# Two heads' attention outputs leave PSUM in one pass instead of two

## The chip, the cores and the metric

The kernel runs on one core of a Trainium2 chip. The metric is the device time of one execution in microseconds; the result is given as the median of several runs. Five engines work side by side, each through its own queue in program order: PE (matrix products into PSUM), DVE (vector), ACT (scalar and activations), POOL (a second, slower vector engine) and SP, which here only issues DMAs. PSUM has eight banks of 512 float32 columns per partition; PE writes its products there, and DVE and ACT read them.

## The reference, cut to what matters

The input x is 1024 x 512. After a layer norm it goes through attention and, beside it, through a gated feed-forward network with 4-bit weights; the result is `x + attention * silu(feed-forward)`. The attention has 32 query heads of 128 columns, which share 8 key and value heads (four query heads each), an RMS norm on queries and keys, and a causal mask with a linear bias:

```
q, k, v = (x @ Wq.T), (x @ Wk.T), (x @ Wv.T)      # 32, 8 and 8 heads of 128
scores  = rmsnorm(q) . rmsnorm(k) / sqrt(128) + slope[head] * (j - i)   # j <= i
attn    = softmax(scores)
out     = (attn . v, all heads side by side) @ Wo.T
```

## The kernel before, in words

To keep float32 accuracy with float16 products, nearly every operand is split into a high and a low float16 half, and a product becomes three: high x high, high x low, low x high (`mm3`, lines 112 to 116, so all such products show as L114, L115 and L116).

The kernel has three stages. The first two, the feed-forward network and the projections of queries, keys and values, take the first half of the span. The third is the attention, and the change lies in it. It works through eight groups g (one key and value head and its four query heads each). Within a group there are four blocks of 256 queries, `qb`; `ORDER` takes them as 2, 3, 0, 1, the first group as 3, 2, 1, 0 and the last as 2, 3, 1, 0. A block has four heads, and one head in one block of queries is a *unit* u, 128 in all, so units 4b to 4b+3 are the heads of block b. Each unit has two tiles of 128 queries, `qt`. Because of the causal mask a tile of block `qb` sees (2 qb + qt + 1) x 128 keys: 128 and 256 in block 0, up to 896 and 1024 in block 3.

The order of the work is written out by hand in `step(n)`, and each engine gets its instructions in that order. Step n takes tile n of the list (unit n // 2, tile n % 2) and the earlier tiles at fixed lags:

- `scores` on PE, tile n, into one of two double banks (tag "s");
- `heads_hi` on ACT, for the unit whose last product with the values was issued one step earlier, that is unit u in step 2u + 11;
- `exponentials`, tile n - 1: on DVE L878 adds the bias to the scores and finds the row extreme, on ACT L879 takes the exponential;
- `split_hi`, tile n - 3: ACT L898 scales the probabilities and rounds them to float16;
- `split_lo`, tile n - 4: DVE L907 makes the low half, and SP issues the DMA (L915, for block 0 L910) that transposes both halves into `pT`;
- `heads_lo` on DVE, for the same unit as `heads_hi`;
- `accumulate` on DVE (L980 mostly), which adds a finished output projection to y;
- `values` on PE, tile n - 9 (`AV_LAG`): the products of `pT` with the values into a bank `av` (tag "o", two banks), with parts of the output projection `out_proj` in between.

So unit u's products with the values are issued in steps 2u + 9 and 2u + 10. `values` takes a new bank when part 0 begins and uses its first 256 columns. In step 2u + 11 the head leaves: `heads_hi` (L941, ACT) writes the float16 half `oh`, 128 x 256, and `heads_lo` (L946, DVE) the remainder `ol`. Both come from pools of `OH_BUFS` = 8 buffers. The output projection of a block whose first unit is u0 begins in step 2u0 + 18 with head 0 and takes one head per step.

Other work shares the queues: the output weights come by DMA (L834), are scaled by POOL (L837), rounded by ACT (L843) and their remainder made by POOL (L844).

Of the kernel before, what the change touches and what calls it, by code (L numbers as in the profile page):

```python
# [12 lines left out]
F16 = mybir.dt.float16  # L13
BF16 = mybir.dt.bfloat16
I32 = mybir.dt.int32
AF = mybir.ActivationFunctionType
ALU = mybir.AluOpType
# [4 lines left out]
P = 128  # L22
# [12 lines left out]
QB = 256  # L35
# [3 lines left out]
P_SCALE = 2.0**14  # L39
# [25 lines left out]
GATE_SUMS = [227, 235, 251, 259]  # L65
PF_BUFS = 5
P16_BUFS = 5
OH_BUFS = 8

_START = 2 ** (-(2 ** (-(math.log2(H) - 3))))  # L70
SLOPES = np.array([_START * _START**i for i in range(H)], dtype=np.float32)
# [5 lines left out]
def attention_gated_by_ffn_kernel(ctx, tc, x, gu_w, gu_z, gu_s, dn_w, dn_z, dn_s, wq, wkv, wo, qnw, knw, out):  # L77
    nc = tc.nc
    ve, se, ge, te, sp = nc.vector, nc.scalar, nc.gpsimd, nc.tensor, nc.sync
# [5 lines left out]
    def ps2(name):  # L85
        return psum[0].tile([P, 2, 512], F32, tag="s", name=name)

    def ps1(tag, name):
        return psum[0].tile([P, 512], F32, tag=tag, name=name)
# [22 lines left out]
    def mm3(ps, lhs, rhs, first, last):  # L112
        (lh, ll), (rh, rl) = lhs, rhs
        te.matmul(ps, lhsT=lh, rhs=rh, start=first, stop=False)  # L114
        te.matmul(ps, lhsT=lh, rhs=rl, start=False, stop=False)  # L115
        te.matmul(ps, lhsT=ll, rhs=rh, start=False, stop=last)  # L116
# [360 lines left out]
    def finish_step():  # L477

        for f in finishing.pop(clock[0], ()):
            f()  # L480
        clock[0] += 1
# [310 lines left out]
    blocks = [(g, qbs) for g in range(HKV) for qbs in (FIRST_ORDER if g == 0 else ORDER if g < HKV - 1 else LAST_ORDER)]  # L792
    units = [(g, qb, hh) for g, qbs in blocks for hh in range(NH) for qb in qbs]
    kT, vT, qT, woh, wol = {}, {}, {}, {}, {}
    trel, pT, oT, wor = {}, {}, {}, {}

    def load_keys(g):
        kT[g] = ap1.tile([P, NT, 2, P], F16, tag="kT", name=f"kT{g}")
        sp.dma_start(kT[g].rearrange("p t a k -> p t (a k)"), kd[g // 2][:, g % 2])

    def load_values(g):
        vT[g] = ap1.tile([P, NT, 2, HD], F16, tag="vT", name=f"vT{g}")
        sp.dma_start(vT[g].rearrange("p t a d -> p t (a d)"), vd[g])

    def load_queries(g, qb):
        qT[g, qb] = ap1.tile([P, NQT, 2, NH, P], F16, tag="qT", name=f"qT{g}_{qb}", bufs=2)
        sp.dma_start(
            qT[g, qb].rearrange("p t a g q -> p t (a g q)"), qd[g][qb * NQT : (qb + 1) * NQT].rearrange("t p c -> p t c")
        )
# [3 lines left out]
    def last_queries(t):  # L813
        g, qb = HKV - 1, t // NQT
        if (g, qb) not in qT:
            qT[g, qb] = ap1.tile([P, NQT, 2, NH, P], F16, tag="qT", name=f"qT{g}_{qb}", bufs=2)
        sp.dma_start_transpose(
            qT[g, qb][:, t % NQT].rearrange("p a g q -> p (a g) q"), last_pairs.pop(t).rearrange("p a g d -> p (a g d)")
        )
# [26 lines left out]
    def relative(g):  # L846

        rel = trel[g] = ap1.tile([P, S], F32, tag="trel", name=f"trel{g}")
        if g == 0:
            ge.iota(rel, pattern=[[-1, S]], base=S - P, channel_multiplier=1, allow_small_or_imprecise_dtypes=True)  # L850
            ge.affine_select(rel, rel, pattern=[[-1, S]], compare_op=ALU.is_ge, fill=1e20, base=S - P, channel_multiplier=1)
            ge.tensor_scalar(rel, rel, rc, float(SLOPES[NH - 1]), ALU.mult, ALU.mult)
        else:
            ge.tensor_scalar(rel, trel[g - 1], float(SLOPES[g * NH + NH - 1] / SLOPES[g * NH - 1]), None, ALU.mult)

    s_ps, pf, rows16, p16, av_ps, op_ps = {}, {}, {}, {}, {}, {}

    def scores(u, qt):
        g, qb, hh = units[u]
        w = (NQT * qb + qt + 1) * P  # L860
        ps = ps2(f"s{u}_{qt}").rearrange("p a c -> p (a c)")
        q = qT[g, qb][:, qt]
        for c0 in range(0, w, 512):
            c1 = min(w, c0 + 512)
            kt = kT[g][:, c0 // P : c1 // P]
            mm3(ps[:, c0:c1], (q[:, 0, hh, :], q[:, 1, hh, :]), (kt[:, :, 0, :], kt[:, :, 1, :]), True, True)
        s_ps[u, qt] = ps[:, :w]
# [51 lines left out]
    def values(u, part, between):  # L919
        g, qb, hh = units[u]  # L920
        nk = NQT * (qb + 1)
        if part == 0:
            av_ps[u] = ps1("o", f"av{u}")[:, :QB]
        ps = av_ps[u]
        per = nk // NQT
        for kt in range(part * per, part * per + per):
            if kt % per == per - 1:
                between()
            c0 = max(0, kt - NQT * qb) * P
            mm3(  # L930
                ps[:, c0:],
                (vT[g][:, kt, 0, :], vT[g][:, kt, 1, :]),
                (pT[u][:, kt, 0, c0:], pT[u][:, kt, 1, c0:]),
                kt == 0,
                kt == nk - 1,
            )

    def heads_hi(u):
        oh = late[0].tile([P, QB], F16, tag="oh", name=f"oh{u}", bufs=OH_BUFS)
        ol = late[0].tile([P, QB], F16, tag="ol", name=f"ol{u}", bufs=OH_BUFS)  # L940
        se.activation(oh, av_ps[u], AF.Copy, scale=1.0 / P_SCALE)  # L941
        oT[units[u]] = (oh, ol)

    def heads_lo(u):
        oh, ol = oT[units[u]]
        ve.scalar_tensor_tensor(ol, av_ps.pop(u), 1.0 / P_SCALE, oh, ALU.mult, ALU.subtract)  # L946

    final = blocks[-1][0], blocks[-1][1][0]

    def out_proj(g, qb, i, part):  # L950
        if part == 0:
            op_ps[g, qb, i] = last_ps[i] if (g, qb) == final else ps1("m", f"op{g}_{qb}_{i}")
        oh, ol = oT[g, qb, part]
        cols = slice(i * P, i * P + P)
        mm3(op_ps[g, qb, i], (oh[:, cols], ol[:, cols]), (woh[g, part], wol[g, part]), part == 0, part == NH - 1)
# [36 lines left out]
    for k, (g, qbs) in enumerate(blocks[:-1]):  # L992
# [5 lines left out]
        n, taken, done = max(free, due), 0, 0  # L998
        op_first.setdefault(g, n)
        for qb in qbs:  # L1000
            for i in range(NQT):
                for part in range(NH):
# [3 lines left out]
                    taken, done = taken + 1, done + 1  # L1006

                    if taken == 2 or n < due + done:
                        n, taken = n + 1, 0
        free = n + (taken > 0)  # L1010
    late, y_ = [], []
    TILES = NT * len(projections)

    def at(n):

        return order[n] if 0 <= n < nn else None

    def step(n):
        nonlocal last_ps
        if n < nn:  # L1020
            u, qt = order[n]
            g, qb, hh = units[u]
            for due in q_at.get(n, ()):
                if due[0] < HKV - 1:
                    load_queries(*due)
            for t, due in LAST_QUERIES.items():
                if due == n:
                    last_queries(t)
            if g + 1 < HKV:
                if n % (NB * BS) == KEYS_STEP:  # L1030
                    relative(g + 1)
                    load_keys(g + 1)
                elif n % (NB * BS) == VALUES_STEP:
                    load_values(g + 1)
            scores(u, qt)
        done = at(n - AV_LAG - 1)
        done = done[0] if done and done[1] == NQT - 1 else None
        if done is not None:
            heads_hi(done)
        for stage, lag in ((exponentials, 1), (split_hi, NQT + 1), (split_lo, NQT + 2)):  # L1040
            if at(n - lag):
                stage(*at(n - lag))
        if done is not None:
            heads_lo(done)
        if n < nn + AV_LAG + 1:
            for due in acc_at.get(n, ()):
                accumulate(*due)
        finish_step()

        def project():  # L1050
            for due in op_at.get(n, ()):
                out_proj(*due)

        if at(n - AV_LAG):
            values(*at(n - AV_LAG), project)
        else:
            project()
        if done is not None and units[done][:2] == final:
            g, qb, hh = units[done]
            if hh == 0:  # L1060
                last_ps = [ps2(f"op_last{i}")[:, 0, :] for i in range(NQT)]
            for i in range(NQT):
                out_proj(g, qb, i, hh)
            if hh == NH - 1:
                for due in acc_at.get(nn + AV_LAG + 1, ()):
                    accumulate(*due, other=True)
                for i in range(NQT):
                    accumulate(g, qb, i)
        if n in GATE_LOADS:
            gate_load(LAST_ORDER[GATE_LOADS.index(n)][0])  # L1070
        for i in range(NQT):
            if n - i in GATE_SUMS:
                gate_partial(LAST_ORDER[GATE_SUMS.index(n - i)][0], i)
        for lead, act in ((WO_SPLIT, split_wo), (WO_SCALE, scale_wo), (WO_LOAD, load_wo)):
            for g, first in op_first.items():
                if n + lead - first in range(0, 2 * NH, 2):
                    act(g, (n + lead - first) // 2)
# [75 lines left out]
```

## Time and profile before

| | |
|---|---|
| three runs, median (lowest to highest) | 1066.62 us (1066.06 to 1070.48) |
| the profiled execution's own time | 1066.42 us |
| its span, first to last instruction | 1064.6 us |
| busy: PE, DVE, ACT, POOL | 1002.7, 886.1, 802.7, 413.9 us |
| exits on ACT, L941 | 128 of 128 x 256, 373 ns each, 47.7 us in all |
| exits on DVE, L946 | 128 of 128 x 256, 418 ns each, 53.5 us in all |
| first and last L941 | 501.2 and 1056.2 us |
| granted clock of PE | 0.993 |

The profile records for every instruction its start and duration, and for idle time before it which event ended it. Its views are a page with shares and slices, groups of instructions by line and shape, windows (busy time of each engine in a stretch), lists of waits, and timelines. Times are counted from the start of the span. An engine's record of an instruction can reach into the next one's, because they are pipelined; where that matters, one counts from start to start. Idle time of an engine that nobody waits for costs nothing.

### The profile page before, as it was taken

The numbers are of one execution on the slowest core, as the hardware profiler recorded it, in microseconds if no ns is written. First come the engines' busy times: TensorE is split into PE (matmuls) and PEld (weight loads), VectorE is DVE, ScalarE is ACT, GpSimd is POOL, SyncE is SP. The second block draws the span as 40 slices with busy tenths as digits, with TensorE's granted clock in tenths as the row PEclk, the third lists the DMA queues.
The fourth block names the chain that finished last, engine by engine and source line by source line (L and its number), as shares of the span: only waits on it lengthen the run. The fifth ranks groups of instructions, "written<-read, shape, count | busy, mean of one in ns | idle before, by whom it ended". The sixth has DMA issues, their size and how long they took to land.

```text
span 1064.6 us, 18405 instructions
## 1 busy us (share of the span) xinstructions
PE 1002.7 (94%) x5913; PEld 584.6 (55%) x5913; DVE 886.1 (83%) x1745; ACT 802.7 (75%) x2160; POOL 413.9 (39%) x407
## 2 busy tenths in 40 slices
PE   7899899999989999898799999999999999999986
PEld 4344377844444444344566666566666666665563
DVE  7888996638778687788799899898998998979986
ACT  5777644778877787587778788797987888868862
POOL 2588653124545546361343215123141141250732
PEclk9999999999999999999999999999999999999998
DMA  6123259447988989989999999899999998999995
GB/s 202 49 100 119 70 170 302 166 139 162 219 228 188 242 203 235 279 179 207 226 193 214 195 200 222 167 227 197 189 207 193 197 223 182 221 224 194 231 189 129
DMA packets 455039, 204.39 MB, mean 192 GB/s; under 512 B 401506, under 2 KB 411038, under 8 KB 454942
## 3 DMA queue, kind: packets, MB, share of 16 engines
q1 hardware_dynamic: 454942, 203.21, 85.4%
q8 instruction: 46, 0.75, 0.3%
q14 instruction: 51, 0.42, 0.1%
HBM read 77.32 MB, written 27.27 MB: 98 GB/s over the span
## 4 chain that ended last, share of the span: by engine, by line
PE 48%; DVE 17%; ACT 13%; issue 10%; DMA 8%; SPq 2%; POOL 2%; DVEq 0%; ACTq 0%; POOLq 0%
PE gu_ps L267 6%; DMA pT<-p 4%; PE s L114 4%; DVE pf L878 3%; PE s L116 3%; PE s L115 3%; PE op L114 3%; PE op L115 3%; PE av L114 3%; PE op L116 3%; PE av L116 3%; PE av L115 3%; ACT p L898 2%; ACT pf L879 2%; PE ps_q L114 2%
## 5 line engine op out<-in xcount | busy, mean ns | idle before, releaser
L907 DVE SCALAR_TENSOR_TENSOR p<-pf,row,p 128x1024 f16<-128x1024 f32 (+7 forms) x256 | 227.8, 890 | 23.5 <-ACT p L898 20.3
L879 ACT ACTIVATE pf<-pf,row 128x1024 f32<-128x1024 f32 (+7 forms) x256 | 197.6, 772 | 57.2 <-DVE row L878 52.7
L878 DVE CUSTOM_DVE_ANT_0 pf<-s,trel,cs 128x1024 f32<-128x1024 f32 (+7 forms) x256 | 207.2, 809 | 13.7 <-PE s L116 13.4
L898 ACT ACTIVATE p<-pf,row 128x1024 f16<-128x1024 f32 (+7 forms) x256 | 196.5, 768 | 8.4 <-DMA pT<-p 3.5
L114 PE MATMUL av<-pT,vT 128*128 128x256 f16 (+1 forms) x640 | 167.8, 262 | 15.5 <-DMA pT<-p 15.5
L115 PE MATMUL av<-pT,vT 128*128 128x256 f16 (+1 forms) x640 | 167.8, 262 | 0.0
L116 PE MATMUL av<-pT,vT 128*128 128x256 f16 (+1 forms) x640 | 167.6, 262 | 0.0
L114 PE MATMUL s<-kT,qT 128*128 128x512 f16 (+3 forms) x384 | 125.0, 325 | 12.4 <-DVE row L878 12.1
L115 PE MATMUL s<-kT,qT 128*128 128x512 f16 (+3 forms) x384 | 125.0, 326 | 0.0
L116 PE MATMUL s<-kT,qT 128*128 128x512 f16 (+3 forms) x384 | 123.4, 326 | 0.0
L837 POOL TENSOR_SCALAR wor<-wor,rvs 128x512 f32<-128x512 f32 x32 | 54.5, 1702 | 162.8 <-DMA wor<-in_wo 141.5
L114 PE MATMUL ps_q<-wh_q,xth 128*128 128x512 f16 x256 | 97.6, 381 | 2.6 <-DVE am_q L526 2.5
L116 PE MATMUL ps_q<-wh_q,xtl 128*128 128x512 f16 x256 | 97.5, 381 | 0.0
L115 PE MATMUL ps_q<-wl_q,xth 128*128 128x512 f16 x256 | 97.5, 381 | 0.0
L114 PE MATMUL op<-woh,oh 128*128 128x512 f16 x248 | 94.5, 381 | 0.0
L115 PE MATMUL op<-wol,oh 128*128 128x512 f16 x248 | 94.3, 380 | 0.0
L116 PE MATMUL op<-woh,ol 128*128 128x512 f16 x248 | 94.2, 380 | 0.0
L114 PEld LDWEIGHTS <-vT 128*128 128x128 f16 x640 | 62.6, 98 | 56.6 <-DMA pT<-p 9.4
L115 PEld LDWEIGHTS <-vT 128*128 128x128 f16 x640 | 62.6, 98 | 41.3 <-issue 3.5
L941 ACT ACTIVATE oh<-av 128x256 f16<-128x256 f32 x128 | 47.7, 373 | 48.5 <-PE av L116 47.8
L636 POOL TENSOR_TENSOR f_q<-f_q,inv_q 128x512 f32<-128x512 f32 x64 | 77.4, 1237 | 1.1
L844 POOL TENSOR_TENSOR wol<-wor,woh 128x512 f16<-128x512 f32 x32 | 49.4, 1543 | 71.3 <-ACT woh L843 71.3
(194 smaller groups left out, 2255.6 us busy)
## 6 DMA issues: line engine op xcount, KB each, us to landing
qd<-tr_q SPq DMA_DIRECT2D x56, 256.0 KB, 3.4
qT<-qd SPq DMA_DIRECT2D x28, 512.0 KB, 4.5
wq<-in_wq SPq DMA_DIRECT2D x32, 256.0 KB, 3.9
wo_sq<-in_wo SPq DMA_DIRECT2D x8, 1024.0 KB, 9.1
wor<-in_wo SPq DMA_DIRECT2D x32, 256.0 KB, 3.7
gui<-in_gu_w SPq DMA_DIRECT2D x13, 512.0 KB, 3.5
wkv<-in_wkv SPq DMA_DIRECT2D x16, 256.0 KB, 3.8
vd<-v SPq DMA_DIRECT2D x8, 512.0 KB, 4.0
```

Source lines behind the costliest of these rows:

```text
L114: te.matmul(ps, lhsT=lh, rhs=rh, start=first, stop=False)
L115: te.matmul(ps, lhsT=lh, rhs=rl, start=False, stop=False)
L116: te.matmul(ps, lhsT=ll, rhs=rh, start=False, stop=last)
L267: te.matmul(banks[j][:, k, :], lhsT=w[:, j, ws], rhs=x[:, j, k * 512 : k * 512 + 512], start=x is xth, stop=x is xtl)
L636: ge.tensor_tensor(f, f, ib, ALU.mult)
L837: ge.tensor_scalar(wor[g, i], wor[g, i], rvs[:, g : g + 1], None, ALU.mult)
L844: ge.tensor_tensor(wol[g, i], raw, woh[g, i], ALU.subtract)
L878: ve.tensor_tensor_reduce(p, ps, trel[g][:, S - w :], cs[:, hh : hh + 1], 3e38, ALU.add, ALU.min, least[:, c])
L879: se.activation(p, p, AF.Exp, bias=least[:, c], scale=-1.0, accum_out=total[:, c])
L898: se.activation(p16[u, qt][:, :, 0, :], pf[u, qt], AF.Copy, scale=scale[:, qt : qt + 1])
L907: ve.scalar_tensor_tensor(lo, p, scale, hi, ALU.mult, ALU.subtract)
L941: se.activation(oh, av_ps[u], AF.Copy, scale=1.0 / P_SCALE)
```

## The change

Two heads of a block, an even unit and the odd one after it, now share a bank: the even unit's product goes to columns 0 to 255, the odd one's to columns 256 to 511. They leave together, after the odd unit's product is done, with one ACT and one DVE instruction of 512 columns each; the even unit's exit in its own step is gone. The four units of the very last block (`final`) stay single, each in a bank of its own with 256 columns. The buffers of `oh` and `ol` become pairs, 6 of 512 columns instead of 8 of 256. `heads_hi` now returns the DVE instruction as a function, which `step` calls where `heads_lo` stood.

```
-OH_BUFS = 8
+OH_BUFS = 6
...
     def values(u, part, between):
...
-        if part == 0:
-            av_ps[u] = ps1("o", f"av{u}")[:, :QB]
-        ps = av_ps[u]
+        if part == 0 and opens(u):
+            av_ps[u] = ps1("o", f"av{u}").rearrange("p (i q) -> p i q", i=2)
+        ps = av_ps[u][:, 0] if opens(u) else av_ps[u - 1][:, 1]
...
+    final = blocks[-1][0], blocks[-1][1][0]
+
+    def opens(u):
+        return u % 2 == 0 or units[u][:2] == final
+
     def heads_hi(u):
-        oh = late[0].tile([P, QB], F16, tag="oh", name=f"oh{u}", bufs=OH_BUFS)
-        ol = late[0].tile([P, QB], F16, tag="ol", name=f"ol{u}", bufs=OH_BUFS)
-        se.activation(oh, av_ps[u], AF.Copy, scale=1.0 / P_SCALE)
-        oT[units[u]] = (oh, ol)
-
-    def heads_lo(u):
-        oh, ol = oT[units[u]]
-        ve.scalar_tensor_tensor(ol, av_ps.pop(u), 1.0 / P_SCALE, oh, ALU.mult, ALU.subtract)
+        n = 1 if opens(u) else 2
+        oh = late[0].tile([P, 2, QB], F16, tag="oh", name=f"oh{u}", bufs=OH_BUFS)[:, :n]
+        ol = late[0].tile([P, 2, QB], F16, tag="ol", name=f"ol{u}", bufs=OH_BUFS)[:, :n]
+        ps = av_ps.pop(u + 1 - n)[:, :n]
+        se.activation(oh, ps, AF.Copy, scale=1.0 / P_SCALE)
+        for i in range(n):
+            oT[units[u + 1 - n + i]] = (oh[:, i], ol[:, i])
+        return lambda: ve.scalar_tensor_tensor(ol, ps, 1.0 / P_SCALE, oh, ALU.mult, ALU.subtract)
...
-        if done is not None:
-            heads_hi(done)
+        heads = done is not None and (done % 2 or units[done][:2] == final)
+        if heads:
+            heads_lo = heads_hi(done)
         for stage, lag in ((exponentials, 1), (split_hi, NQT + 1), (split_lo, NQT + 2)):
             if at(n - lag):
                 stage(*at(n - lag))
-        if done is not None:
-            heads_lo(done)
+        if heads:
+            heads_lo()
```

More of the change, by code (lines that the diff above doesn't have):

```diff
@@ L936, in values @@
             )
+    final = blocks[-1][0], blocks[-1][1][0]
+    def opens(u):
+        return u % 2 == 0 or units[u][:2] == final
     def heads_hi(u):
-        oh = late[0].tile([P, QB], F16, tag="oh", name=f"oh{u}", bufs=OH_BUFS)
-        ol = late[0].tile([P, QB], F16, tag="ol", name=f"ol{u}", bufs=OH_BUFS)
-        se.activation(oh, av_ps[u], AF.Copy, scale=1.0 / P_SCALE)
-        oT[units[u]] = (oh, ol)
-    def heads_lo(u):
-        oh, ol = oT[units[u]]
-        ve.scalar_tensor_tensor(ol, av_ps.pop(u), 1.0 / P_SCALE, oh, ALU.mult, ALU.subtract)
-    final = blocks[-1][0], blocks[-1][1][0]
+        n = 1 if opens(u) else 2
[6 more added lines that the diff above has]
+        return lambda: ve.scalar_tensor_tensor(ol, ps, 1.0 / P_SCALE, oh, ALU.mult, ALU.subtract)
     def out_proj(g, qb, i, part):
```

## The prediction

> **What bounds the kernel now.** I read the page first: engine shares, and the span in 40 slices.
>
> ```profile
> PE   7899899999989999898799999999999999999986
> DVE  7888996638778687788799899898998998979986
> ```
>
> The change touches only the attention stage, from the first heads at 501 us to the end: the right half, where PE and DVE both stand near full. So next came the windows of one of its eight groups, group 3, cut at the steps where its key width changes (768, 1024, 256, 512 columns).
>
> ```profile
> 685.50:702.00 16.50, 16.50 (x117) 10.47 (x116) 16.21 (x35) 15.07 (x33) 2.76 (x1) 1.00 1.05 207
> 702.00:725.10 23.10, 23.10 (x159) 14.63 (x158) 22.43 (x38) 19.82 (x35) 10.33 (x6) 1.00 1.07 218
> 725.10:741.30 16.20, 15.23 (x125) 11.27 (x124) 12.53 (x36) 12.44 (x37) 5.51 (x7) 1.00 1.06 195
> 741.30:754.80 13.50, 13.50 (x89) 7.75 (x87) 12.08 (x35) 10.87 (x30) 0.39 (x1) 1.00 0.76 179
> ```
>
> After the stretch's length come PE, PEld, DVE, ACT and POOL busy. PE is full in three blocks out of four; in the third it is idle 0.97 us. The start times of its matmuls say 1.4 us, since the recorded ends overlap. PE is the bound, and only its waits can be won. They are, over groups 1 to 6 (546 to 960 us), in the list of waits:
>
> ```profile
> PE s L114 <- DVE row L878: 5.5, 11, 0.7
> PE av L114 <- DMA pT<-p: 3.1, 3, 1.4
> ```
>
> (us in total, times, longest.) Before 546 us there are 0.3 and 5.9 us of the same two kinds, after 960 us 1.9 and 6.5: 23 us in all. This is the most that any relief of ACT and DVE can return. Where the first kind arises is seen in the timelines of DVE, PE and ACT around the third block of group 3.
>
> ```profile
> 712.73 1.15 DVE L878 CUSTOM_DVE_ANT_0 pf<-s,trel,cs 128x896 f32<-128x896 f32 x1 [0.31 <-PE s L116]
> ...
> 715.07 0.42 DVE L946 SCALAR_TENSOR_TENSOR ol<-av,oh 128x256 f16<-128x256 f32 x1
> 715.50 1.28 DVE L878 CUSTOM_DVE_ANT_0 pf<-s,trel,cs 128x1024 f32<-128x1024 f32 x1
> ...
> 722.48 0.41 DVE L946 SCALAR_TENSOR_TENSOR ol<-av,oh 128x256 f16<-128x256 f32 x1
> 722.82 1.27 DVE L878 CUSTOM_DVE_ANT_0 pf<-s,trel,cs 128x1024 f32<-128x1024 f32 x1
> ...
> 727.65 0.42 DVE L946 SCALAR_TENSOR_TENSOR ol<-av,oh 128x256 f16<-128x256 f32 x1
> ...
> 728.78 1.57 DVE L907 SCALAR_TENSOR_TENSOR p<-pf,row,p 128x896 f16<-128x896 f32 x1 [0.32 <-ACT p L898]
> 730.28 0.74 DVE L980 SCALAR_TENSOR_TENSOR y<-op,isg,y 128x512 f32<-128x512 f32 x1
> ...
> 731.29 1.98 DVE L907 SCALAR_TENSOR_TENSOR p<-pf,row,p 128x1024 f16<-128x1024 f32 x1
> 733.19 0.41 DVE L946 SCALAR_TENSOR_TENSOR ol<-av,oh 128x256 f16<-128x256 f32 x1
> 733.52 0.47 DVE L878 CUSTOM_DVE_ANT_0 pf<-s,trel,cs 128x256 f32<-128x256 f32 x1
> ```
>
> ```profile
> 731.34 0.22 PE L114 MATMUL s<-kT,qT 128*128 128x128 f16 x1 [0.38 <-DVE row L878]
> 734.05 0.27 PE L114 MATMUL s<-kT,qT 128*128 128x256 f16 x1 [0.59 <-DVE row L878]
> ```
>
> ```profile
> 726.32 0.60 ACT L843 CAST woh<-wor 128x512 f16<-128x512 f32 x1
> 726.83 0.37 ACT L941 ACTIVATE oh<-av 128x256 f16<-128x256 f32 x1
> 727.10 0.39 ACT L879 ACTIVATE pf<-pf,row 128x128 f32<-128x128 f32 x1
> ```
>
> In the 1024-wide block DVE falls behind; from 712.73 to 733.9 it never waits for PE. When the narrow block begins, PE has to wait for L878 to free a bank of scores, last at 734.05. DVE's lateness at that moment is the one number through which the change can reach the end.
>
> **The change, part by part.** 124 of the 128 single exits become 62 pairs of 512 columns; four stay single. In each pair the even unit's exit disappears from its step, and the odd unit's, two steps later, doubles.
>
> *One exit.* Records overlap their successors, so I count start to start. DVE: a 256-wide L946 takes 0.33 (733.19 to 733.52). A 512-wide one is not in the trace: L878's rows grow from 474 to 742 ns between 256 and 512 columns, hence 0.33 + 0.27 = 0.60; L980, also 512 wide out of PSUM, takes 0.66 (730.28 to the next start at 730.94) and is the upper end. I take 0.60, since L980 writes float32. By recorded durations a pair would give 2 x 418 - 686 = 150 ns. ACT: 0.27 for 256 (726.83 to 727.10); for 512 columns 0.27 plus 256 x 0.82 ns (the slope of L898's rows, 402 to 1134 ns from 128 to 1024), so 0.48, beside the 0.51 of the 512-wide L843. Per pair DVE saves 0.06 (0 to 0.15) and ACT 0.06; over 62 pairs 3.7 us each (DVE 0 to 9.3). Nearly all lies beside PE's full blocks, at no gain.
>
> *On the path: DVE's shift against before in group 3* (+ is later). At 712.73 DVE waits 0.31 for PE: shift 0. 715.07, odd: +0.27. 722.48, even, gone: -0.33, so -0.06. 727.65, odd: +0.27, so +0.21. At 728.78 DVE already waits 0.32 for ACT, whose pair at 726.83 takes 0.21 more; with the -0.06 that ACT inherited the product starts at +0.15. 733.19, even, gone: -0.33, so -0.18. The scores at 734.05 come at 733.87, and PE, full from there, keeps 0.18 us. Groups 1 to 6 share this pattern (5.5 us of waits). But three of them wait again, on the transposed probabilities (3.1 us), and those are issued behind the wide L907 at 731.29 that has moved by +0.15. So groups 1, 3, 4: -0.54; groups 2, 5, 6: +0.45.
>
> *Group 0.* Its 5.9 us of waits hang on the output weights (casts on L843 wait 3.9 us for POOL); after the last such cast, at 519.40, comes an odd exit (+0.21) and then a vanished even one (-0.27 on ACT): -0.06.
>
> *Group 7.* DVE is behind for three pairs, at -0.06 each: -0.18. The last block is single as before.
>
> *Waits at no cost.* A pair's bank was left four steps before its reuse (now two), and no wait of PE for L946 to free a bank is listed. The output projection reads an even head five steps after the pair's exit, where seven were; steps of 1.7 us (13.50/8) give 8 us for exits of about 1. Six pair buffers reach back 12 units; the last block's third single takes the buffer of units 116 and 117, read until step 257, at step 263. SP and POOL keep every instruction and their order; no DMA is added. ACT's waits for PE at the even exits (about half of 37 us) vanish; they lie where PE is full, and DVE next waits for PE's scores instead.
>
> Sum: -0.54 + 0.45 - 0.06 - 0.18 = -0.33. The profiled execution took 1066.42 us (span 1064.6), 0.2 below the median of 1066.62: forecast **1066.1**.
>
> Start to start, a merged pair saves DVE 0.06 us by the rows above, and none of PE's listed waits is for an exit to free a bank. [...]
>
> **The rivals.** *Faster: the entry waits go.* In one stretch the same 128x1024 L907 takes 1.26 us (713.88) and 1.98 (731.29), 1.82 (720.74), the longer ones while POOL's L844 runs. If the shifted order lets two of them run alone, DVE is 1.3 us earlier per group, which is more than PE's longest wait at an entry, 0.7. All 5.5 us in groups 1 to 6 and 1 of the 1.9 later would go, -6.5: 1059.9. Against: POOL follows ACT's casts, which move by only 0.2. It counts as faster from 5.3 us on.
>
> *Slower: pairs delay the transposes.* The odd step puts +0.27 on DVE and +0.21 on ACT ahead of the next L907. Where PE already waits for pT (14 waits, 15.5 us) both could add up: 14 x 0.48 = +6.7, 1073.1. It decides from 0.38 per wait. For: those waits have no slack. Against: only wide L907s behind an odd exit suffer, and half stand behind an even one.
>
> *The change doesn't deliver:* if 512 columns cost 0.66, the pair saves nothing and the walk ends at -0.06 per group instead of -0.18: 1066.5, in the first case's range.
>
> **How the numbers follow.** 0.5% of this kernel, 5.3 us, is about what a measurement of it tells from no change. First case 0.68, its own range 1064.0 (recorded durations: -0.30 more per group) to 1068.5 (+0.3 on each of eight groups, both terms in series). Faster 0.18, slower 0.14. To leave out at most 2 in 10 the range takes about 40% of each: 1060.5 to 1072.0.
>
> **What would show it.** L941 and L946's successors: 62 rows of 512 columns at about 0.58 and 0.69 us recorded, and four of 256. The period of groups 3 to 5 (69.3 us) within 0.3 us of before; PE's waits for L878 in 546 to 960 near 4.5 to 6 us; those for pT near 3 to 4. Wrong would be: L907's mean of 1510 ns at 1024 columns falling or rising by 0.2 us (POOL), or pT waits over 20 us in total.

## The result, and the profile after

The changed kernel takes 1078.01 us (median of five; 1074.05 to 1082.53), the kernel before 1068.48 us beside it (1066.06 to 1070.48): a ratio of 1.0097, 95% interval 1.0077 to 1.0117 (a figure over all the runs; the two medians alone give 1.0089). It is slower by about 1%, where no change was forecast (1066.1, range 1060.5 to 1072.0). The profiled execution took 1081.18 us, so its trace shows rather more of the loss than the median.

The page of the changed kernel, shares and the two slice rows:

```profile
PE 1008.0 (93%) x5913; PEld 586.2 (54%) x5913; DVE 881.2 (82%) x1683; ACT 796.0 (74%) x2098; POOL 411.4 (38%) x407
...
PE   7899899999999899897899999998999999989986
...
DVE  7888996538777787788789797996997989969975
```

and the groups of instructions, shapes kept apart, for the pair exits:

```profile
L952 DVE SCALAR_TENSOR_TENSOR ol<-av,oh 128x512 f16<-128x512 f32 x62 | 42.6, 686 | 16.3 <-ACT oh L949 16.3
...
L949 ACT ACTIVATE oh<-av 128x512 f16<-128x512 f32 x62 | 36.0, 581 | 37.8 <-PE av L116 37.8
```

The change did what it says: 62 pairs of 686 and 581 ns, and DVE and ACT have 4.9 and 6.7 us less to do than before (886.1 and 802.7). The span grew all the same. The windows of group 3, cut at the same steps as the four rows shown of before (length, PE, PEld, DVE, ACT, POOL, clock, DMA share, GB/s):

```profile
689.70:706.10 16.40, 16.40 (x116) 10.30 (x115) 16.11 (x34) 14.05 (x28) 1.41 (x1) 1.00 0.95 201
706.10:728.10 22.00, 22.00 (x150) 13.93 (x149) 21.72 (x35) 19.23 (x33) 9.61 (x6) 1.00 1.09 207
728.10:750.00 21.90, 18.09 (x133) 12.59 (x131) 13.05 (x37) 12.24 (x35) 5.57 (x7) 0.92 1.05 197
750.00:763.80 13.80, 13.80 (x89) 7.74 (x88) 11.81 (x29) 11.57 (x31) 1.34 (x1) 1.00 0.63 137
```

The two wide blocks became shorter, the 1024-wide one from 23.10 to 22.00 us. The third became 5.7 us longer (16.20 to 21.90): PE stands idle 3.8 us there, and part of it ran at a lower clock. What PE waits for in groups 1 to 6 (548 to 971 us), from the list of waits (us in total, times, longest):

```profile
ACT oh L949 <- PE av L116: 32.6, 7, 7.8
DVE pf L878 <- PE s L116: 28.6, 13, 6.8
...
PE av L114 <- DMA pT<-p: 9.9, 6, 3.3
...
PE s L114 <- DVE row L878: 3.2, 10, 0.7
```

The waits that the change could win fell from 5.5 to 3.2 us. Those for the transposed probabilities rose from 3.1 to 9.9. Each of the six lies at the same place, the first product of the group's last wide unit (unit 16g + 7): 0.68, 1.87, 3.26, 0.73, 0.42 and 2.94 us in groups 1 to 6, against 0, 1.05, 0, 0.05, 0.66 and 1.38. Group 7 and the end, from 960 us on, went from 6.5 to 9.6 us of the same wait. ACT and DVE wait longer for PE because PE itself is late.

From the starts of the groups' first L878, the profiled executions differ by 14.8 us: 1.9 before the first group, +0.2, +1.9, +0.2, +4.9, +0.1, -0.1 and +2.2 in groups 0 to 6, +3.5 from group 7 to the end. The 1.9 us ahead of the attention can't be put down to the exits: in the 15 traces of kernels with the same start, the two here among them, the first L878 comes anywhere from 448.8 to 453.3 us. The two longest of the waits in groups 1 to 6 (3.26 and 2.94 us) cost twice, for behind each the granted clock was 0.51. The windows there, in groups 3 and 6 (same columns):

```profile
744.90:748.40 3.50, 3.50 (x15) 2.05 (x16) 0.00 (x0) 0.00 (x0) 0.00 (x0) 0.51 0.90 236
956.50:960.00 3.50, 3.19 (x13) 1.82 (x14) 0.00 (x0) 0.00 (x0) 3.35 (x4) 0.51 1.10 320
```

### The profile page after: what moved, and what is told of

It is laid out like the page before. It is cut to its first block, busy times and chain, and to the rows that moved or that the text cites. A ratio compares the mean times of both kernels' runs of the same rounds, so it can differ in the third digit from the quotient of the medians.

```text
span 1079.4 us, 18260 instructions
## 1 busy us (share of the span) xinstructions
PE 1008.0 (93%) x5913; PEld 586.2 (54%) x5913; DVE 881.2 (82%) x1683; ACT 796.0 (74%) x2098; POOL 411.4 (38%) x407
## 5 line engine op out<-in xcount | busy, mean ns | idle before, releaser
L907 DVE SCALAR_TENSOR_TENSOR p<-pf,row,p 128x1024 f16<-128x1024 f32 (+7 forms) x256 | 227.6, 889 | 26.8 <-ACT p L898 24.4
L878 DVE CUSTOM_DVE_ANT_0 pf<-s,trel,cs 128x1024 f32<-128x1024 f32 (+7 forms) x256 | 207.3, 810 | 30.5 <-PE s L116 30.3
L114 PE MATMUL av<-pT,vT 128*128 128x256 f16 (+1 forms) x640 | 168.9, 264 | 25.5 <-DMA pT<-p 25.5
L837 POOL TENSOR_SCALAR wor<-wor,rvs 128x512 f32<-128x512 f32 x32 | 57.1, 1784 | 174.9 <-DMA wor<-in_wo 153.3
L949 ACT ACTIVATE oh<-av 128x512 f16<-128x512 f32 (+1 forms) x66 | 37.5, 569 | 50.2 <-PE av L116 50.2
L844 POOL TENSOR_TENSOR wol<-wor,woh 128x512 f16<-128x512 f32 x32 | 46.3, 1448 | 62.8 <-ACT woh L843 62.8
```

Source lines behind the costliest of these rows:

```text
L837: ge.tensor_scalar(wor[g, i], wor[g, i], rvs[:, g : g + 1], None, ALU.mult)
L844: ge.tensor_tensor(wol[g, i], raw, woh[g, i], ALU.subtract)
L878: ve.tensor_tensor_reduce(p, ps, trel[g][:, S - w :], cs[:, hh : hh + 1], 3e38, ALU.add, ALU.min, least[:, c])
L907: ve.scalar_tensor_tensor(lo, p, scale, hi, ALU.mult, ALU.subtract)
L949: se.activation(oh, ps, AF.Copy, scale=1.0 / P_SCALE)
```

## The experiments

"Waits" below is PE's wait for transposed probabilities from 501 to 1060 us in the one profiled execution of each kernel (before 15.5, changed 25.5); one execution each, so a difference of 2 us says little (before and e10 differ by 1.8 at the same time). "Lead" is the time from the end of the L907 on a group's first wide tile to the first product that reads it, from start times in the trace, in groups 3 to 5 (before 10.80, changed 9.55). Ratios are to the kernel before, beside which each kernel was run.

| kernel | ratio [95%] | waits, us | lead, us |
|---|---|---|---|
| changed | 1.0097 [1.0077, 1.0117] | 25.5 | 9.55 |
| e1 two exits of 256 for one of 512 | 1.0070 [1.0052, 1.0088] | 23.5 | 9.55 |
| e2 pair exit a step later | 1.0110 [1.0091, 1.0130] | 24.5 | 9.31 |
| e3 changed, third table buffer | 1.0057 [1.0036, 1.0078] | 22.7 | 10.29 |
| e4 before, third table buffer | 0.9993 [0.9978, 1.0009] | 18.1 | 10.81 |
| e5 pairs in wide blocks only | 1.0014 [0.9997, 1.0030] | 22.9 | 10.45 |
| e6 pairs in narrow blocks only | 1.0004 [0.9991, 1.0018] | 16.0 | 9.88 |
| e7 before, ten steps | 0.9960 [0.9944, 0.9975] | 3.4 | 12.58 |
| e8 changed, ten steps | 0.9982 [0.9969, 0.9994] | 9.8 | 12.32 |
| e9 changed, weights earlier | 1.0043 [1.0025, 1.0061] | 21.8 | 9.31 |
| e10 before, weights earlier | 1.0000 [0.9988, 1.0013] | 17.3 | 10.60 |
| e11 before, two more L907 | 1.0023 [1.0012, 1.0034] | 13.6 | 9.08 |
| e12 before, ten steps, weights earlier | 0.9942 [0.9923, 0.9960] | 9.3 | 12.25 |
| e13 changed, program loads shifted | 1.0025 [1.0010, 1.0040] | 17.6 | 9.55 |
| e14 before, program loads shifted | 0.9994 [0.9980, 1.0008] | 13.3 | 10.81 |
| e15 e13 with third table buffer | 1.0010 [0.9997, 1.0022] | 18.8 | 10.29 |
| e16 changed, ten steps, weights earlier | 0.9982 [0.9970, 0.9994] | 6.2 | 11.62 |
| e17 changed, shifted by a whole period | 1.0100 [1.0075, 1.0126] | 21.8 | 9.55 |
| e18 e12 with program loads shifted | 0.9958 [0.9943, 0.9973] | 3.8 | 12.26 |

### The form of the exit: two of 256, and a step later (e1, e2)

```
# e1
-        se.activation(oh, ps, AF.Copy, scale=1.0 / P_SCALE)
         for i in range(n):
+            se.activation(oh[:, i], ps[:, i], AF.Copy, scale=1.0 / P_SCALE)
...
# e2
+        exit = at(n - AV_LAG - 2)
+        exit = exit[0] if exit and exit[1] == NQT - 1 and exit[0] % 2 and units[exit[0]][:2] != final else None
```

> The pair leaves as two 256-wide exits on each engine instead of one 512-wide, in the same odd steps and out of the same shared bank: what differs from the changed kernel is the width alone, what differs from the kernel before is the bank and the step of the even exit. Theory 'step' (the even exit two steps later shifts ScalarE's and VectorE's queues against TensorE and the transposes): 1.010 of before, as the changed kernel, or up to 1.013, for VectorE has some 31 x 0.16 = 5 us more to do than in the changed kernel. Rival 'pace' (VectorE's 5 us less work in the wide blocks lets transposes pile up in the DMA queue): 1.000 to 1.003, the pacing being back. If the width alone cost the time: 1.000.

> The changed kernel with each pair's exit one step later, so that ScalarE doesn't reach it before TensorE has done the odd head's product. Theory 'head of line' (ScalarE's queue stands up to 7.8 us at the exit behind TensorE's product, and the exponentials behind it are late): most of the loss goes, 1.000 to 1.004 of before, and ScalarE's waits for the products fall from 38 us (20 to 1060 us) to under 15 us. Rival 'lead' (the wide block's first transposes are issued about 1.25 us later against TensorE, and ScalarE's long waits only follow from TensorE's own stall): 1.007 to 1.012, with TensorE's waits for transposes near 25 us as in the changed kernel.

Two exits of 256 columns out of the shared bank lose nearly as much, 1.0070 (the medians, 1077.80 and 1078.01 us, hardly differ): the width is not what costs most of it. A step later, ACT's waits for PE's products before the 62 pair exits fall from 37.8 to 0.6 us, and the kernel is no faster, 1.0110. So the theory of the head of ACT's queue falls: the loss stays without that wait.

### A collision on POOL (e3, e4)

DVE and POOL where group 3 begins, in timelines of the kernel before, of the changed one and of e3. L854 scales the distance table for the next group (`relative`), once a group, as soon as DVE has read the old table for the last time:

```profile
685.01 0.61 DVE L907 SCALAR_TENSOR_TENSOR p<-pf,row,p 128x384 f16<-128x384 f32 x1
...
685.19 3.07 POOL L854 TENSOR_SCALAR trel<-trel 128x1024 f32<-128x1024 f32 x1 [17.77 <-DVE row L878]
```

```profile
688.33 2.77 POOL L854 TENSOR_SCALAR trel<-trel 128x1024 f32<-128x1024 f32 x1 [18.08 <-DVE row L878]
688.41 1.37 DVE L907 SCALAR_TENSOR_TENSOR p<-pf,row,p 128x384 f16<-128x384 f32 x1 [0.17 <-ACT p L898]
```

```profile
686.91 0.62 DVE L907 SCALAR_TENSOR_TENSOR p<-pf,row,p 128x384 f16<-128x384 f32 x1 [0.17 <-ACT p L898]
```

In the changed kernel the even exit that stood just ahead of this last read of the table is gone (before, L946 at 684.01). DVE reaches the L907 earlier, waits 0.17 us for ACT, POOL's L854 gets in first by 0.08 us, and L907 takes 1.37 instead of 0.61 us. This happens in each of groups 2 to 6 and takes 0.75 of the 1.25 us of lost lead. With a third buffer L854 doesn't wait, and so doesn't meet that L907:

```
-        rel = trel[g] = ap1.tile([P, S], F32, tag="trel", name=f"trel{g}")
+        rel = trel[g] = ap1.tile([P, S], F32, tag="trel", name=f"trel{g}", bufs=3)
```

> The changed kernel with a third buffer for the distance table that GpSimd scales once a group, so that its 3 us instruction no longer waits for VectorE's last read of the old table and doesn't run beside the first wide subtraction (0.61 us before, 1.37 us with the changed kernel, once a group). Theory 'collision' (that stretched subtraction takes the lead of the first wide transposes): 0.61 us again for that subtraction, TensorE's waits for transposes back near 16 us, 1.001 to 1.005 of before. Rival 'step' or 'pace': 1.008 to 1.012, the subtraction being short but the waits staying.

> The kernel before with the same third buffer, as the control of the run above. Theory 'collision': 0.998 to 1.001 of before, for there the two instructions didn't meet. If the third buffer helps or harms by itself (the table scaled at another time, beside other VectorE work), this run shows it: then 0.995 or 1.005, and the run above has to be read against this one.

The subtraction is at 0.62 us again and the lead at 10.29. The ratio falls to 1.0057, the control stays at 0.9993: the collision has a share in this kernel's loss, though the waits, at 22.7 us, are not back near 16 as expected. By itself it costs nothing, as the next section shows.

In groups 2 to 6 alike the one that began second was the one stretched. Before, L907 came first by 0.18 us, kept its 0.61 (0.62 in group 2), and L854 took 3.07. In the changed kernel L854 came first by 0.08 us, took 2.77, and L907 took 1.37. L907, second there, didn't wait until L854 had ended: in group 3 it ended at 689.78, L854 1.3 us later.

### Pairs in one half of the blocks (e5, e6)

```
+    def single(u):
+        return units[u][:2] == final or units[u][1] not in (2, 3)      # e6: not in (0, 1)
     def opens(u):
-        return u % 2 == 0 or units[u][:2] == final
+        return u % 2 == 0 or single(u)
```

The condition in `step` uses `single` too, and `OH_BUFS` is 8.

> Pairs only where a row block has 768 to 1024 keys (the wide blocks); the heads of the narrow blocks leave singly, as before. The narrow heads' exits are what VectorE and ScalarE do just ahead of the next group's first wide transpose, so this run gives that transpose its old place (10.80 us ahead of its product; 9.55 in the changed kernel) and keeps the pairs behind it. Theory 'lead' (the wide block's transposes come at the DMA queues' rate, about 45 us from the first issue to the last landing, so that each us by which the first is later is up to a us of stall at the group's last wide product): 0.999 to 1.003 of before. Rival 'pace' (the faster exits inside the wide block pile up transposes): 1.005 to 1.010.

> The other half: pairs only where a row block has 128 to 512 keys, single exits in the wide blocks. Theory 'lead': 1.006 to 1.010, near the whole of the loss, with the first wide transpose near 9.5 us ahead of its product. Rival 'pace': 0.999 to 1.003.

Neither half costs anything that can be told from nothing, 1.0014 and 1.0004; the two together cost 0.97%. By "lead" e6 should have carried nearly all of it. It has the collision on POOL too, in each of groups 2 to 6; where group 3 begins:

```profile
687.25 2.77 POOL L854 TENSOR_SCALAR trel<-trel 128x1024 f32<-128x1024 f32 x1 [17.01 <-DVE row L878]
687.33 1.37 DVE L907 SCALAR_TENSOR_TENSOR p<-pf,row,p 128x384 f16<-128x384 f32 x1 [0.17 <-ACT p L898]
```

So a lead shorter by 0.9 us, 0.75 of it by the collision, costs nothing as long as the wide blocks keep single exits. Nor are the 8 buffers here instead of 6 the difference: all that the changed kernel's exits wait for is PE's product (ACT, 37.8 us) and ACT's half (DVE, 16.3). The loss is not a sum over the pairs: something has room that either half leaves, and both together don't. (The profiled execution of e5, 1074.82 us, was the longest of its twelve, so its 22.9 us of waits are above its usual.)

### More room: ten steps, fewer loads; and less (e7 to e11)

```
-AV_LAG = 9
+AV_LAG = 10                                        # e7, e8
...
+                early = 18 if act is load_wo and g else 0           # e9, e10
-                if n + lead - first in range(0, 2 * NH, 2):
-                    act(g, (n + lead - first) // 2)
+                if n + lead + early - first in range(0, 2 * NH, 2):
+                    act(g, (n + lead + early - first) // 2)
...
+        if 1 < units[u][0] < HKV - 1 and u % 16 == 0 and qt == 0:   # e11
+            idle = late[0].tile([P, NT, P], F16, tag="idle", name=f"idle{u}", bufs=1)
+            for _ in range(2):
+                ve.scalar_tensor_tensor(idle[:, :nk], p, scale, hi, ALU.mult, ALU.subtract)
```

> The kernel before with the products with the values one step later behind the scores (ten steps instead of nine). It gives every transpose a step more, in the wide blocks 2 us and more. Theory 'lead': TensorE's waits for transposes, 15.5 us after 501 us, fall below 8 us, and the time to 0.990 to 0.997 of before, if nothing else is in the way; the last block then ends a step later, some 1 us. Rival (the waits are the DMA queues' rate alone, and a longer lead only moves them to the transposes' buffers): 0.998 to 1.004.

> The changed kernel with the same ten steps. Theory 'lead': what the change cost was lead, so with a step to spare it costs little: within 0.003 of the run above. Rival 'pace' or any cost of the pairs on TensorE's path itself: 0.006 to 0.010 above the run above.

> The changed kernel with the four 256 KB loads of the output weights of groups 1 to 7 moved 18 steps earlier, out of the wide blocks (where the 16 DMA engines stand idle for 5 to 10% of the time) into the narrow ones just before (idle 25 to 40%). It takes 1.05 of some 9.4 MB from the stretch in which the wide transposes have to land, some 4.8 us at the 218 GB/s of those slices. Theory 'budget' (the wide transposes come at the DMA engines' rate; the lead of the first one is their whole slack, and the change took 1.25 us of it): the waits at the groups' last wide products, 0.4 to 3.3 us in groups 1 to 6, fall below 0.5 us, and the time to 0.995 to 1.001 of before, within 0.003 of the run below. Rival (the pairs cost time on the engines' own path, whatever the transposes do): 0.006 or more above the run below.

> The kernel before with the same earlier loads, the control of the run above. Theory 'budget': its own waits at those products, 0 to 1.4 us a group, go too: 0.994 to 0.998 of before. If the loads were not what the transposes share the DMA engines with: 0.999 to 1.001.

> The kernel before with two more VectorE subtractions of 128x768 (some 0.9 us each by the rows of that form) ahead of the first wide one of groups 2 to 6: it takes some 1.8 us from the lead of the wide transposes and touches no exit. Theory 'budget': the lead falls from 10.80 to about 9.0 us, and waits of about 1 us come at the last wide product of each of the five groups: 1.004 to 1.009. Rival (the lead is slack, and it is the pairs' own place that costs): 0.999 to 1.002.

A step more between transposes and products makes both kernels faster and leaves 0.2% between them (0.9982 to 0.9960) instead of 1.0%. So about three quarters of the loss go with a step more of room for the transposes. The waits themselves follow less closely (PE from 501 to 1060 us, e7 and then e8):

```profile
PE s L114 <- DVE row L878: 12.1, 22, 2.1
PE av L114 <- DMA pT<-p: 3.4, 4, 1.6
```

```profile
PE s L114 <- DVE row L878: 12.8, 24, 2.1
PE av L114 <- DMA pT<-p: 9.8, 8, 2.7
```

With pairs there are still 6.4 us more of the waits for transposes, though the two profiled executions differ by 0.4 us (1065.25 and 1065.61). Taking the output weights' loads out of the wide blocks gave the changed kernel 0.5% and the kernel before nothing, where 0.2 to 0.6% had been expected; and the waits at the last wide products didn't vanish (1.56, 1.75 and 0.70 us in groups 2 to 4). The extra subtractions (of 128 x 640, where 128 x 768 had been announced), 0.89 us each, took 1.72 us of lead from the kernel before, more than the change does, and its waits fell to 13.6 us; the 0.23% that it costs lies elsewhere. The run is not a clean test: PE too was ready for the last wide product some 0.7 us later (35.1 to 35.3 us after the first wide product in groups 2 to 5, 34.4 to 34.6 before), which gave the transposes more time. With e6 it is enough to say that a shorter lead alone is not the cause. Whatever makes the transposes late is not only how early the first one is issued, nor only how many bytes pass beside them.

### Program loads (e13 to e15, e17)

The trace records every DMA packet, those of the engines' own programs too: 46 loads of 16 KB in one queue, one for some 256 of PE's instruction records on average. The DMA view of the changed kernel around the last wide transposes of group 3 (738.6 to 745.0 us), in 40 slices of 0.16 us (busy tenths of the DMA engines, GB/s, then the queues: packets, MB, share; at the end the transposes' time from issue to landing):

```profile
DMA  9995999999999998009999999900000002999999
GB/s 336 278 198 120 253 291 290 290 291 290 290 311 267 272 126 40 10 14 269 293 290 288 389 272 270 214 0 0 6 8 8 11 8 51 257 291 291 254 288 285
...
q8 instruction: 1, 0.02, 0.9%
q14 instruction: 1, 0.01, 0.4%
...
pT<-p SPq DMA_TRANSPOSE x3, 6.1
```

and the same stretch of the kernel before (732.4 to 738.8 us), also up to just past the product's start:

```profile
DMA  9999879999989999999999999999999800069999
GB/s 371 397 307 282 205 282 358 368 314 307 259 138 229 288 293 290 288 293 290 274 285 293 122 283 296 290 285 296 282 266 253 166 3 0 0 146 224 221 211 210
...
pT<-p SPq DMA_TRANSPOSE x4, 4.8
```

In the changed kernel the transposes come to a stop from 742.8 to 744.0 us: 0 to 11 GB/s, where 290 went before and after. The 16 KB load began at 742.2; a shorter stop, 741.0 to 741.5 us, follows an 8 KB load at 740.4. In the kernel before, no program load falls into this stretch (the next begins 1 us after PE has started the product), and the short gap near its end (737.5 to 738.0 us) is the end of the last wide transpose, which lands at 738.02.

This is no single case. Over the wide blocks of groups 1 to 6 in all 20 traces, the 2.5 us after the start of a 16 KB load hold about 1.1 us (median of 243) at under 40 GB/s, after an 8 KB load of the other program queue 0.5 us (184), and stretches of 2.5 us without any load a median of at most 0.1 us (some 1200). It is plainest for the last wide transpose of a group, from its issue to its landing, or to the product that waited for it: 4.24 to 4.56 us in the 58 cases without a program load, 5.26 to 6.79 us in the 45 where a 16 KB load begins between 1 us ahead of the issue and 0.5 us ahead of the landing. The kernel before has both kinds too: 5.8 and 5.6 us in groups 2 and 6, where it waits, 4.3 to 4.5 in the others.

If the 16 KB loads follow the count of PE's instructions, adding some at the start moves them against the work (it did: the one in group 2, 31.1 us after the first wide product in the changed kernel, came at 22.3 with the edit of e13). At the start PE has only the transposes into `warm` to do (40 in the kernel before, 1.36 to 8.15 us):

```
-    for i in range(WARM):
+    for i in range(WARM - 12):                     # e17: WARM - 20
         te.transpose(warm[:, :P], ident, ident)
+    for i in range(62):                            # e17: 148, of 64 columns
+        te.matmul(warm[:, :P], lhsT=ones_bf, rhs=ones_bf, start=True, stop=True)
```

> The changed kernel with 12 of the 40 warm-up transposes at the very start replaced by 62 short products of a constant: about 110 more TensorE instructions, in time in which TensorE has nothing to do, and with that every later 16 KB load of TensorE's program (256 instructions, 19.5 us apart in the wide blocks) comes some 8 us earlier against the work. Counted from the first wide product of a group, the loads at 31.1, 35.0 and 32.2 us in groups 2, 3 and 6 go to about 23, 27 and 24, and that at 37.6 in group 4 to about 31. Theory 'program load' (such a load on the same DMA engines makes the last wide transposes land 1 to 2 us later): the wait at the last wide product falls by 1 us or more in group 3 (3.26 us) and by about 1 in groups 2 and 6 (1.87 and 2.94), and rises by about 1 in group 4 (0.73); 1.003 to 1.007 of before. Rival (the load only stands beside it): groups 2, 3 and 6 keep their waits, 1.008 to 1.012.

> The kernel before with the same extra instructions. Theory 'program load': groups 2 and 6 (1.05 and 1.38 us) lose about 1 us each, group 4 gains about 1: 0.997 to 1.000 of before. Rival: no group moves, 0.999 to 1.001.

> The changed kernel with the third table buffer and the shifted program loads. If the two effects add (1.0057 with the buffer alone): 1.000 to 1.003 of before. If the buffer's gain and the shift's are the same one: as the better of the two alone, 1.004 to 1.006.

> The changed kernel with 20 of the 40 warm-up transposes replaced by 148 short products: 256 more TensorE instructions by the records, one whole period of the 16 KB program loads, so that these fall at the same places of the attention as in the changed kernel, though the start differs as in the shifted run. Theory 'program load': the loss comes back, 1.007 to 1.011 of before. Rival (the altered start gave the gain of the shifted run): 1.001 to 1.004, as there.

The shift (100 records by the trace) takes three quarters of the loss away: 1.0025. The kernel before doesn't care: 0.9994. A shift by a whole period of 256 puts the loads back (31.0, 33.8 and 31.6 us after the first wide product in groups 2, 3 and 6, as against 31.1, 35.0 and 32.2 in the changed kernel), and the loss is back, 1.0100. So the altered start is not what helped. How much of the 1.0100 it costs isn't known, as no run puts the same 148 products into the kernel before: in the profiled execution the first L878 comes at 453.7 us, 3.1 us later than before, and the time from there to the end is 6.3 us longer (1.7 with the shift of 100, 12.9 in the changed kernel). PE's waits from 501 to 1060 us with the shift of 100:

```profile
PE av L114 <- DMA pT<-p: 17.6, 16, 4.3
PE s L114 <- DVE row L880: 3.2, 11, 0.4
```

and with the shift of 256:

```profile
PE av L114 <- DMA pT<-p: 21.8, 16, 2.7
PE s L114 <- DVE row L880: 6.9, 13, 1.8
```

At the last wide products e13 has 1.57, 1.42, 1.17 and 1.68 us in groups 2, 3, 4 and 6: group 3 lost 1.8 and group 6 lost 1.3, group 4, into which a load moved (32.3 us), gained 0.4; group 2 lost only 0.3, though its load moved to 22.3 us. In group 6 the last wide transpose lands sooner, 4.4 us after its issue instead of 5.6. In group 3 it doesn't: a load, now at 30.9 us, still falls beside it (6.1 us both times), and what fell is the delay of its issue, from 2.3 us behind its L907 to 0.5. So in groups 1 to 6 the loads explain a part. The clearest place is group 7: in the changed kernel loads begin 3.4 and 3.5 us ahead of the products of its units 7 and 12, which wait 1.93 and 2.71 us; with the shift of 100 these waits are nothing and 0.22 us, with that of 256 they are 2.13 and 2.14. From 960 us on e13 has 6.1 us for 9.6. In the kernel before the waits follow the loads as well: groups 2 and 6 lose 0.5 and 0.6 us, groups 3 and 4, where loads now come at 31.8 and 31.5 us, gain 0.6 each; the sum over groups 1 to 6 hardly changes (3.1 and 2.5 us).

With the third table buffer besides (e15) 1.0010 is left, which can't be told from no change. The two effects overlap: the buffer gives 0.4% where the loads lie badly; the 0.15% where they don't lies within the intervals.

### A faster kernel (e12, e16, e18)

These join edits shown above.

> The kernel before with both: ten steps between scores and products, and the earlier loads. Theory 'budget': with the waits already gone by either one, both together give little more than the better of the two, 0.992 to 0.996 of before. If other waits stand behind them, they show here.

> The changed kernel with ten steps between scores and products and the output weights loaded 18 steps earlier: the counterpart of the run that gave 0.9942 of before with single exits. If the pairs cost only by way of the transposes: within 0.001 of that, 0.993 to 0.9955, or below it by what the pairs save (VectorE and ScalarE some 4 to 5 us each, off the path). If they cost on the path itself: 0.996 or more, as between the two runs with ten steps alone (0.996 and 0.998).

> The kernel before with ten steps, the earlier loads of the output weights (0.9942 of before with both) and the program loads shifted by some 100 instructions. There little waiting for transposes is left (5.4 us in groups 1 to 7 against 9.6), so by theory 'program load' the shift gives little: 0.993 to 0.996.

The kernel before with ten steps and the earlier loads takes 0.9942 of its time (1062.02 us), faster than both kernels. Its waits of PE from 501 to 1060 us:

```profile
PE s L114 <- DVE row L878: 11.4, 22, 1.9
PE av L114 <- DMA pT<-p: 9.3, 9, 2.3
```

Shifted program loads add nothing to it (0.9958, intervals overlapping). With pairs it is 0.9982, 0.4% behind, where 0.1% at most was expected if the pairs cost only by way of the transposes, and 0.996 or more if they cost on the engines' own path; the transposes' waits are fewer there (6.2 us), so this part of the pairs' cost is another one. In e16 PE waits 18.4 us for L878 from 440 to 1064 us, in e12 15.1; that is a pointer and no proof, and what it is stays open.

## Why the prediction was wrong

- **The exits' price was right.** 0.58 and 0.69 us recorded were forecast; 0.58 and 0.69 they are. From start to start, 0.48 and 0.60 us were forecast, and the medians are 0.48 and 0.60.
- **The gain at the entry of the narrow block came in sum.** It was put at 0.18 us for each of groups 1 to 6. From the first wide product of a group to PE's being ready for that of the last wide unit, the changed kernel is 0.11, 0.62, 0.06, 0.60, -0.08 and 0.00 us quicker. But in group 4, the clearest (33.95 us instead of 34.55), PE then waits 0.73 us for the transposes, before 0.05. In the forecast groups 1, 3 and 4 kept the gain because they showed no such wait; they had little reserve behind it: in groups 1 and 3 the last wide transpose had landed 0.1 and 0.6 us ahead of the product.
- **The step that failed: "SP and POOL keep every instruction and their order; no DMA is added", put at nothing, and with it the term of +0.15 us for the transposes of groups 2, 5 and 6.** A transpose was taken to land a fixed time behind its L907. It doesn't: in group 3 the last wide one landed 4.8 us after the end of its L907 before (733.26 to 738.02) and 8.4 after (736.36 to 744.77). One part is the way from issue to landing, 4.3 and 6.1 us; over all 20 traces it was 4.24 to 4.56 us where no program load fell beside the transpose and 5.26 to 6.79 beside a 16 KB load of PE's program, and no line of the forecast had these loads, although the page lists them as "instruction" packets. The other part is the issue itself, 0.5 and 2.3 us behind the L907, because SP was still issuing the transposes ahead of it; in group 6 this part alone grew (1.4 to 2.8 us). For groups 1 to 6 the term was +0.45 in sum; measured are +6.8 us of waits (3.1 to 9.9) in the profiled executions, where the last wide transposes were issued 3.9 us later in sum and took 2.0 us longer to land. What made SP late in this execution isn't shown; with the loads at nearly the same places (e17) it was 0.8 us in group 3, not 2.3.
- **DVE's shift walk stopped too late in the group.** It followed the exits into the narrow block. It left out the entry of the wide one: with the even exit gone, a wait of 0.17 us for ACT let POOL's L854 begin ahead of an L907, which took 0.75 us more. Alone that costs nothing (e6); with pairs in the wide blocks as well it has a share (e3). The order of POOL's queue was kept, as the forecast said; its moment against DVE was not.
- **Group 7's -0.18 us.** From its first L878 to the end the changed kernel took 3.5 us more; shifting the loads brought that stretch from 101.88 to 98.84 us (98.35 before).
- **The rival "pairs delay the transposes"** had the right place, PE's waits for pT, and a chance of 0.14. It was priced at 14 x 0.48 = 6.7 us, from the exits' lengths; 9.5 us came (medians), but three quarters of it go when only the program loads are moved and every exit stays (e13). "Faster" and "doesn't deliver" fall.
- **Of the two signs named for a wrong forecast** one was there: pT waits over 20 us (25.5). L907's mean at 1024 columns went from 1510 to 1421 ns, less than the 0.2 us named, and in the good direction; it bought nothing. Of the signs for a right one, the period held in groups 4 and 5 (69.5 and 69.9 us; 69.4 and 70.0 before) and not in group 3 (74.1; 69.2).

Shown by the runs: that a step more of room for the transposes takes most of the loss away (e8), that in the changed kernel the place of the program loads makes about three quarters of it (e13, e17; one shift each, and the start of e17 uncontrolled), and that the last wide transpose takes 5.26 to 6.79 us with a 16 KB program load beside it, 4.24 to 4.56 without a program load. The collision on POOL has a part, in the changed kernel alone (e3, against e6). Argued only: why the program loads cost the changed kernel more than the kernel before. The kernel before waits beside them too (groups 2 and 6), and moving them there moved the waits to groups 3 and 4 and left the time alone. With pairs in the wide blocks PE is ready earlier in some groups (33.95 instead of 34.55 us in group 4, e5 too), with pairs in the narrow ones the transposes begin later; that each half alone is free (e5, e6) fits a reserve that both together use up, but how much reserve there is was not measured. And 0.2 to 0.4% of the pairs' cost stays where little waiting for transposes is left (e8, e16); its cause is open.

## What to carry to other kernels

Where a product waits for a DMA that lands just in time, an edit that frees other engines may win nothing (here 4.9 us of DVE and 6.7 of ACT), and shifts of a us within a block can add up to a per cent (0.97% here); give that DMA a step more room first (here 0.4% by itself). A difference of 1% between two kernels whose instructions differ can be, in good part, the place of the program loads (here 1.0097 became 1.0025 by moving them): before it is put down to the edit, shift one engine's instruction stream by some hundred cheap instructions in both kernels and see whether the difference stays. When costing an edit, list also what POOL runs beside the moved DVE instructions, since here the one that began second was stretched (L907 to 1.37 us from 0.61, 0.08 us behind POOL; L854 to 3.07 from 2.77, 0.18 us behind DVE).

## What the runs showed of the hardware

- In the 2.5 us after the start of a 16 KB load of PE's program (one for some 256 instruction records) the DMA engines move under 40 GB/s for about 1.1 us (median of 243 loads; down to 0 to 11 GB/s from 290 in the one shown), after an 8 KB one for 0.5. The last wide transpose of a group takes 4.24 to 4.56 us without a load beside it, 5.26 to 6.79 with a 16 KB one. Why a load of 16 KB holds up the whole queue the trace doesn't show.
- L907 of 384 columns beside POOL's L854: 1.37 instead of 0.61 us when POOL began 0.08 us ahead; L854 3.07 instead of 2.77 us when L907 began 0.18 us ahead. Neither waited for the other's end: L907 as the second ended 1.3 us ahead of L854, and L854 as the second 2.64 us after L907 (group 3), less than its own 2.77. Nearer than that the recorded starts don't tell which is stretched: ahead by 0.05 us (changed kernel, 472.56) an L907 of 896 columns took 2.03 us, ahead by 0.06 (before, 470.71) 1.15.
- Around the end of PE waits of 3.3 and 2.9 us (groups 3 and 6) the granted clock fell to half for 3.41 us, by the clock's own records, some 1.7 us of work lost each time by estimate (half of 3.41).
